# A gated delta layer on one NeuronCore: the TensorE order of a slot written as a list, and two products moved to four 64x64 tiles

## The chip, the cores and the metric

The program runs on one core of a Trainium2 chip. All data is float32. The metric is the device time of one execution in microseconds (us); the kernel before is given by the median of three runs.

## What is computed

Two layers over 2 sequences of 1024 tokens, 256 channels each. Layer 0 adds a gated delta rule and a mixture of experts to the stream; layer 1 adds a gated linear attention and a sparse unit. Nearly all the time goes to the delta rule of layer 0, and the change is there. Cut to what matters:

```python
qkvz = hidden_states @ W_qkvz                 # 16 key heads; each feeds 2 of the 32 value heads
q, k, v = silu(conv4(q, k, v))                # causal, 4 taps, per channel
q, k = l2norm(q) * 128**-0.5, l2norm(k)
def step(S, inp):                             # S: 128 x 128 per value head
    qt, kt, vt, gt, bt = inp
    S = S * exp(gt)
    delta = (vt - kt @ S) * bt
    S = S + outer(kt, delta)
    return S, qt @ S
gated = core * silu(z)
out = rms_norm(gated) * norm_w @ W_out
```

## The kernel before

Tokens of both sequences share the 128 partitions: the lower 64 hold 64 tokens of sequence 0, the upper 64 the same tokens of sequence 1. Such a block of 64 + 64 tokens is a chunk; there are 16 along the sequence. Heads go in 8 groups of four value heads (two key heads, `m` = 0 and 1, with two value heads `i` each), one group after the other, so there are 128 chunks of work. Two chunks make a pair (64 pairs), four a unit.

Inside a chunk the recurrence is solved in matrix form (`chunk_state`, L733): `pks`, `pqs` = keys and queries times the state (L748); DVE folds `pks` into the value tokens `vtok` (L751); `pf` = the inverted 64x64 triangle `invT` times `vtok` (L766), copied by ACT to `f` (L768); `pS` = keys times `f`, added to the state `S` by DVE (L775, L786); `po` = the query scores `np[:, 1]` times `f` (L779), added by DVE to `qs` (L790) and multiplied by the gate `z` (L792). ACT then takes four sums of squares (`gsq`, L797), POOL makes the norm's factors and multiplies (`chunk_output`, L807 to L814), and TensorE transposes and projects (`yT` L818, `out` L830). In `pf` the stationary and moving tensors span all 128 partitions: `invT` is a 128x128 matrix with the two sequences' 64x64 blocks on its diagonal and zeros elsewhere. `po` runs on two 64x64 tiles of the array, sequence 0 in the lower corner, sequence 1 in the upper. `pS` runs on all four.

The tokens' side (`chunk_tokens`, L707): TensorE transposes keys (`pk`) and values (`pv`), ACT copies the keys to `kt` (L716), and one POOL instruction scales them for four heads into `ktok` (L720).

The triangle of a pair is made in three steps spread over two slots. `pair_scores` (L521): DVE scans the decays (L540), ACT takes the exponential (L542), POOL multiplies (`lb`, L544), TensorE makes the scores `kq` (L552), DVE multiplies into `np` (L558; index 0 for the triangle, 1 for the outputs). SP then issues the DMAs that lay `np[:, 0]` out anew: `nat` (4, L562), `natd` to DRAM (2, L568) and from there `n` (8, L572). `pair_lanes` (L576): a chain of small DVE instructions inverts the 8x8 blocks of `n` (L590 to L612), ending in `E` (L614), which two DMAs turn into `U` by way of DRAM (`ed` L616, `U` L618). `pair_inverse` (L642), one slot later: DVE transposes `U` to `L` (L663); then twice TensorE `px`, ACT `xs`, TensorE `pyt` (L635), DVE `U` and `L` (L675, L677) join the blocks to 32x32, and once more `px`, `xs`, `pyt` (L692 to L703) to 64x64 in `invT`.

The work is a software pipeline over slots, one slot per pair: slot `p` makes the scores and lanes of pair `p`, the inverse of pair `p - 1`, both chunk states of pair `p - 2`, the last output of pair `p - 3`, and four blocks of projection and convolution (`conv_block`, L328: TensorE `pj`, ACT two copies L357 and L359, DVE three taps L376, ACT the silu L386). What sets the order of a slot is `in_windows` (L855): every piece of work is a generator with a window of the slot, and the piece whose next step is due first is advanced. A scheduler of the recording layer then orders each engine's instructions and puts in the semaphores; it follows these priorities but may exchange instructions that do not depend on each other. Engines take their instructions in order. SP's queue holds nearly all DMA issues, in one order as well, each waiting there for its data.

PSUM is one pool of eight banks, taken in turn by every product (`ps_tile`, L67).

Of the kernel before, what the change touches and what calls it, by code (L numbers as in the profile page):

```python
# [14 lines left out]
P = 128  # L15
D = 256
KT = D // P
NB = 2
# [162 lines left out]
def delta_gates(k, pool, I):  # L181
# [66 lines left out]
    for b, rows in enumerate((LO, HI)):  # L248
        ps = ps_tile(k, f"sum_end{b}")
        nc.tensor.matmul(ps, k.ones[rows], flat(g)[rows], start=True, stop=True)  # L250
        nc.scalar.activation(flat(k.eEnd[:, b]), ps, AF.Exp)
        yield
# [136 lines left out]

def conv_part(k, pools, p, n, count):  # L390

    u, odd = divmod(p, 2)
    blocks = []
    if odd:
        blocks = [(u + 1, 1, 0), (u + 1, 1, 1), (u + 1, 0, 2), (u + 1, 0, 3)]
    else:
        blocks = [(u + 1, 0, 0), (u + 1, 0, 1), (u, 1, 2), (u, 1, 3)]
    for v, m, i in blocks[n : n + count]:  # L400
        if 0 <= v < NUNIT:
            yield from conv_block(k, pools, k.units[v], m, i)
        elif k.projected:
            yield from convolve(k)
            silu_pending(k)
# [115 lines left out]
def pair_scores(k, pools, pr):  # L521

    nc, wk, h = k.nc, pools.work, pr.h
    pr.nat = wk.tile([P, PC, HPG, B], F32, tag="nat32", name=f"nat32{pr.name}")
    pr.n8 = wk.tile([P, W, W], F32, tag="n8", name=f"n8{pr.name}")

    lb, c0 = pr.g, pr.chunks[0].c
    flat = lb.rearrange("p x h i -> p (x h i)")
    with k.tc.issue_after(k.anchor):
        nc.vector.tensor_tensor_scan(flat, flat, k.floor, -200.0, ALU.add, ALU.max)  # L540
    yield
    nc.scalar.activation(flat, flat, AF.Exp)  # L542
    yield
    nc.gpsimd.tensor_tensor(lb, lb, bcast(h.nb[:, c0 : c0 + PC], 3, CT), ALU.mult)  # L544
    yield

    kq = ps_tile(k, f"kq{pr.name}").rearrange("p (x m s i) -> p x m s i", x=PC, m=KPG, s=2)
    for x in pr.chunks:
        for m in range(KPG):
            for b, rows in enumerate((LO, HI)):  # L550
                both = of_chunk(h.kq[m], x.c, b)
                nc.tensor.matmul(kq[rows, x.at, m], both[:, 0], both, start=True, stop=True)  # L552
    yield
    pr.np = pools.np.tile([P, 2, PC, HPG, CT], F32, tag="np", name=f"np{pr.name}")
    pairs = lambda a: a.rearrange("p x (m j) i -> p (x m) j i", m=KPG)
    for s in range(2):
        by = kq[:, :, :, s].rearrange("p x m i -> p (x m) i")
        nc.vector.tensor_tensor(pairs(pr.np[:, s]), pairs(lb), bcast(by, 2, 2), ALU.mult)  # L558
        if s == 0:
            yield  # L560
    for n, r in enumerate(QUARTERS):
        nc.sync.dma_start(pr.nat[r], pr.np[r, 0, :, :, QUARTERS[n % 2]])  # L562


    step = W * (PH * CT + 1)
    nd = k.dram.tile([NB, CT // W * step], F32, tag="nat", name=f"natd{pr.name}", bufs=2)
    for b, rows in enumerate((LO, HI)):
        nc.sync.dma_start(nd[b, 0 : CT * PH * CT].rearrange("(j c) -> j c", j=CT), pr.np[rows, 0].rearrange("p x h i -> p (x h i)"))  # L568
    for a in range(PH):
        at = slice(a * (P // W), (a + 1) * (P // W))  # L570
        src = bass.AP(nd.tensor, nd.offset + a * CT, [[step, P // W], [PH * CT, W], [1, W]])
        nc.sync.dma_start(pr.n8[at], src)  # L572
    yield
# [68 lines left out]
def pair_inverse(k, pools, pr):  # L642
# [42 lines left out]
    for n, r in enumerate(QUARTERS):  # L685
        (nc.gpsimd.tensor_copy, nc.scalar.copy)[n % 2](invT[r, :, r], U[r])
    yield
# [14 lines left out]
    for q, copy in ((0, nc.scalar.copy), (2, nc.vector.tensor_copy)):  # L702
        copy(invT[QUARTERS[q], :, QUARTERS[q + 1]], pyt[QUARTERS[q]])  # L703
    yield


def chunk_tokens(k, pools, x):  # L707

    nc, wk, h, c = k.nc, pools.work, x.h, x.c
    if not x.last:  # L710
# [6 lines left out]
        x.k = wk.tile([P, HPG, P], F32, tag="ktok", name=f"ktok{x.name}")  # L717
        pair = lambda a: a.rearrange("p (m i) c -> p m i c", m=KPG)
        wend = h.wend[:, c, :].rearrange("p (m i) -> p m i", m=KPG)
        nc.gpsimd.tensor_tensor(pair(x.k), bcast(kt, 2, 2), bcast(wend, 3, P), ALU.mult)  # L720
        yield
# [11 lines left out]
def chunk_state(k, pools, x):  # L733

    nc, wk, h, c = k.nc, pools.work, x.h, x.c
    t = h.t0 + c
# [4 lines left out]
    if not x.first:  # L741
        pks, pqs = four(k, f"pks{x.name}"), four(k, f"pqs{x.name}")
        for s, out in ((0, pks), (1, pqs)):
            for m in range(KPG):
                two = slice(2 * m, 2 * m + 2)
                for b, rows in halves:
                    q = of_chunk(h.kq[m][:, s], c, b)
                    nc.tensor.matmul(out[rows, two, :], q, k.S[:, b, two, :], start=True, stop=True)  # L748
        yield
# [13 lines left out]

    pf = four(k, f"pf{x.name}")
    for i in range(HPG):
        nc.tensor.matmul(pf[:, i, :], invT[:, i, :], x.v[:, i, :], start=True, stop=True)  # L766
    f = wk.tile([P, HPG, P], F32, tag="f", name=f"f{x.name}")
    nc.scalar.copy(f, pf)  # L768
    yield
    if not x.last:  # L770
        pS = [four(k, f"pS{x.name}_{b}") for b in range(NB)]
        for i in range(HPG):
            for b, rows in halves:
                for cols in (LO, HI):
                    nc.tensor.matmul(pS[b][cols, i, :], x.k[rows, i, cols], f[rows, i, :], start=True, stop=True)  # L775
    po = four(k, f"po{x.name}")
    for i in range(HPG):
        for b, rows in halves:
            nc.tensor.matmul(po[rows, i, :], x.pair.np[rows, 1, x.at, i, :], f[rows, i, :], start=True, stop=True)  # L779
    yield  # L780
# [6 lines left out]
    yield  # L787
    no = po
    if not x.first:
        nc.vector.tensor_tensor(qs, qs, po, ALU.add)  # L790
        no = qs
    nc.vector.tensor_tensor(x.z, no, x.z, ALU.mult)  # L792
    yield
# [77 lines left out]


def delta_layer(k, I):
    nc, tc = k.nc, k.tc
    with ExitStack() as ctx:
# [11 lines left out]
        k.tails = const.tile([P, 4 * KPG, NB, KSIZE - 1], F32, tag="tails", name="tails")  # L887
        k.invT = [const.tile([P, PC, HPG, P], F32, tag=f"invT{i}", name=f"invT{i}") for i in range(2)]

# [35 lines left out]
        for p in range(-2, NPAIR + 3):  # L925


            work = []
            add = lambda kind, lo, hi, steps, *before: work.append((kind, lo, hi, steps, before))
            prefetch(k, pools, p)  # L930
            if p == -2:
                for q in (0, 1):
                    pair_decays(k, pools, pair(q))
            add("conv0", 0.0, 0.475, conv_part(k, pools, p, 0, 2))
            add("conv1", 0.475, 0.71, conv_part(k, pools, p, 2, 1), "conv0")
            add("conv2", 0.71, 0.95, conv_part(k, pools, p, 3, 1), "conv1")
            add(f"gates{p % 2}", 0.65, 1.0, gates_part(k, pools, p), "output1", "conv1")
            if pair(p):
                add("scores", 0.0, 0.45, pair_scores(k, pools, pair(p)))
                add("lanes", 0.65, 0.9, pair_lanes(k, pools, pair(p)), "scores")  # L940
            if pair(p - 1):
                add("inverse", 0.0, 1.0, pair_inverse(k, pools, pair(p - 1)))
                add("tokens0", 0.5, 1.0, chunk_tokens(k, pools, pair(p - 1).chunks[0]), "state0")
            if pair(p - 2):
                one, two = pair(p - 2).chunks
                add("tokens1", 0.0, 0.4, chunk_tokens(k, pools, two))
                add("state0", 0.0, 0.5, chunk_state(k, pools, one))
                add("state1", 0.5, 1.0, chunk_state(k, pools, two), "state0", "tokens1")
                add("output0", 0.55, 1.0, chunk_output(k, pools, one), "state0")
            if pair(p - 3):  # L950
                one, two = pair(p - 3).chunks
                add("output1", 0.05, 0.5, chunk_output(k, pools, two))
                add("project0", 0.05, 0.4, chunk_project(k, pools, one))
                add("project1", 0.55, 0.9, chunk_project(k, pools, two), "output1")
            in_windows(k, *work)
            if pair(p) and pair(p + 2):
# [433 lines left out]
def two_layers(ctx, tc, I, out):  # L1390
# [3 lines left out]
    k.keep = ctx.enter_context(tc.tile_pool(name="keep", bufs=1))  # L1394
    k.psum = ctx.enter_context(tc.tile_pool(name="psum", bufs=8, space=bass.MemoryType.PSUM))

# [8 lines left out]
    k.xnT = k.keep.tile([P, KT, N], F32, tag="xnT", name="xnT")  # L1405

    with tc.tile_pool(name="ln0", bufs=2) as pool:
        tiles = {}
# [10 lines left out]
    with ExitStack() as scope:  # L1419
        k.gates = scope.enter_context(tc.tile_pool(name="d_gates", bufs=1))  # L1420
        k.dram = scope.enter_context(tc.tile_pool(name="d_dram", bufs=1, space=bass.MemoryType.DRAM))
        expert_layer(k, I)
        delta_layer(k, I)

    with ExitStack() as scope:
        pool = lambda name, bufs: scope.enter_context(tc.tile_pool(name=name, bufs=bufs))
        pools = Pools()
        pools.const, pools.work, pools.h = pool("l1_const", 1), pool("l1_work", 2), pool("l1_h", 2)
# [68 lines left out]
```

## Time and profile before

| | us |
|---|---|
| median of 3 runs (lowest, highest) | 2921.37 (2916.87, 2931.51) |
| the profiled execution, its time | 2925.03 |
| its span, first to last instruction | 2923.3 |
| first `pj` of the delta stage, from the timeline | 268.2 |
| last `out` of the delta stage | 2616.4 |
| first `kq` of slot 4, of slot 61, and 57 slots between | 420.7, 2468.1, 35.9 each |

PE is TensorE's matmuls, PEld its weight loads, DVE VectorE, ACT ScalarE, POOL GpSimd, SP the engine whose queue issues DMAs. A group's row has its line, engine, operation, output <- inputs, shape and count; then the union of its busy time in us, the mean of one instruction in ns, and the idle time of its engine before it with what ended it. A float32 matmul is two records, so counts are twice those of the source. Matmuls of different tiles overlap, so the busy time over the count is the price of one, and the mean is not.

### The profile page before, as it was taken

What the parts mean: (1) busy time and instruction counts of PE and PEld (TensorE: products, weight loads), DVE (VectorE), ACT (ScalarE), POOL (GpSimd) and SP (SyncE); (2) the same over time, 40 slices, a digit from 0 to 9 for tenths busy, and PEclk for the clock granted to TensorE, in tenths of its full rate; (3) what the DMA queues carried; (4) which work ended last, traced back from release to release, by engine and by line L of the source; (5) the groups of instructions that cost most, each with busy time, mean ns of one, the idle gap of its engine ahead of it and who ended that gap; (6) DMA issues with size and microseconds to landing.
All of it is one profiled execution on the core that took longest, in us unless ns stands there. A gap on an engine that the chain in (4) does not pass through costs nothing.

```text
span 2923.3 us, 87736 instructions
## 1 busy us (share of the span) xinstructions
PE 2657.6 (91%) x36502; PEld 1676.2 (57%) x36502; DVE 2000.5 (68%) x3845; ACT 1717.9 (59%) x4121; POOL 1608.1 (55%) x2690
## 2 busy tenths in 40 slices
PE   5998699999999999999999999999999999889997
PEld 2444455666566566656665666556665666554565
DVE  7653667777777777777767777777677777545544
ACT  4432666676666666766666667666666666544321
POOL 2222566676666666766676667666766666530000
PEclk9999899999999999999999999999999999999999
DMA  3001111111112111111111112111111111110000
GB/s 77 4 1 58 37 28 35 36 44 26 42 29 46 28 43 35 36 28 43 35 38 26 43 36 45 25 42 37 38 28 35 29 29 28 21 60 0 1 15 15
DMA packets 265965, 95.22 MB, mean 33 GB/s; under 512 B 220512, under 2 KB 244192, under 8 KB 265568
## 3 DMA queue, kind: packets, MB, share of 16 engines
q1 hardware_dynamic: 261872, 86.67, 13.3%
q8 instruction: 287, 4.70, 0.7%
q10 hardware_dynamic: 3696, 2.95, 0.4%
q14 instruction: 110, 0.90, 0.1%
HBM read 53.63 MB, written 27.53 MB: 28 GB/s over the span
## 4 chain that ended last, share of the span: by engine, by line
PE 55%; DVE 21%; POOL 9%; issue 6%; ACT 5%; DMA 3%; SPq 2%; DVEq 0%; ACTq 0%; POOLq 0%
PE pj L152 10%; DVE conv L376 5%; PE out L830 5%; PE z L152 3%; PE pks L748 3%; PE px L635 3%; PE pS L775 2%; PE pf L766 2%; PE pqs L748 2%; DVE S L786 2%; PE y L1115 2%; PE pg L152 2%; PE base L152 2%; DVE np L558 2%; POOL rn L479 2%
## 5 line engine op out<-in xcount | busy, mean ns | idle before, releaser
L376 DVE SCALAR_TENSOR_TENSOR conv<-raw,convw,conv 128x512 f32<-128x512 f32 x768 | 697.1, 938 | 22.2 <-ACT conv L359 18.7
L152 PE MATMUL pj<-xnT,w 128*128 128x512 f32 x1024 | 531.2, 645 | 9.4 <-DMA w<-in_W_qkvz 9.4
L797 ACT ACTIVATE gsq<-z 128x128 f32<-128x128 f32 x512 | 157.4, 307 | 352.3 <-DVE z L792 319.8
L756 POOL TENSOR_TENSOR S<-S,eEnd 128x512 f32<-128x512 f32 x224 | 274.4, 1244 | 75.8 <-PE pqs L748 46.0
L152 PEld LDWEIGHTS pj<-xnT,w 128*128 128x128 f32 x1024 | 192.4, 201 | 195.7 <-issue 186.5
L751 DVE SCALAR_TENSOR_TENSOR vtok<-pks,neG,vtok 128x128 f32<-128x128 f32 x480 | 135.2, 344 | 189.6 <-PE pks L748 188.7
L152 PE MATMUL z<-wz,xnT 128*128 128x512 f32 x512 | 260.3, 633 | 0.0
L830 PE MATMUL out<-wo,yTs 128*128 128x256 f32 x1024 | 250.7, 388 | 1.4 <-ACT yTs L820 1.4
L357 ACT COPY raw<-pj 128x512 f32<-128x512 f32 x256 | 146.3, 572 | 120.8 <-PE pj L152 81.1
L786 DVE TENSOR_TENSOR S<-S,pS 128x512 f32<-128x512 f32 x224 | 145.5, 682 | 84.6 <-POOL S L756 55.0
L830 PEld LDWEIGHTS out<-wo,yTs 128*128 128x128 f32 x1024 | 185.7, 191 | 25.6 <-ACT yTs L820 2.0
L635 PE MATMUL px<-L,natm 32*32 32x32 f32 x8192 | 99.8, 197 | 90.4 <-DVE L L677 73.5
L359 ACT ACTIVATE conv<-pj,convw 128x512 f32<-128x512 f32 x256 | 176.1, 688 | 0.0
L361 POOL COPY tails<-raw 128x6 f32<-128x6 f32 x192 | 52.0, 271 | 223.8 <-ACT raw L357 180.9
L386 ACT ACTIVATE v<-conv 128x512 f32<-128x512 f32 x128 | 81.1, 634 | 149.0 <-DVE conv L376 149.0
L761 ACT ACTIVATE qs<-pqs,neG 128x128 f32<-128x128 f32 x480 | 136.0, 362 | 42.9 <-PE pqs L748 42.8
L479 POOL TENSOR_TENSOR rn<-sse,mhalf 128x16 f32<-128x16 f32 x32 | 93.0, 2906 | 115.9 <-DVE sse L492 115.9
L635 PEld LDWEIGHTS px<-L,natm 32*32 32x32 f32 x8192 | 85.8, 108 | 115.9 <-DVE L L677 55.8
L807 POOL TENSOR_TENSOR ms<-sumsq,q 128x4 f32<-128x4 f32 x128 | 61.5, 480 | 160.8 <-ACT gsq L797 160.8
L720 POOL TENSOR_TENSOR ktok<-kt,wend 128x512 f32<-128x512 f32 x120 | 149.7, 1247 | 0.1
L152 PEld LDWEIGHTS z<-wz,xnT 128*128 128x128 f32 x512 | 92.5, 195 | 96.0 <-issue 72.9
L766 PE MATMUL pf<-vtok,invT 128*128 128x128 f32 x1024 | 143.9, 284 | 3.3 <-DVE vtok L751 3.3
(323 smaller groups left out, 6120.9 us busy)
## 6 DMA issues: line engine op xcount, KB each, us to landing
lb<-grows SPq DMA_DIRECT2D x128, 128.0 KB
natd<-np SPq DMA_DIRECT2D x128, 128.0 KB
w<-in_W_qkvz SPq DMA_DIRECT2D x16, 512.0 KB
nat<-np SPq DMA_DIRECT2D x256, 32.0 KB
n<-natd SPq DMA_DIRECT2D x512, 4.0 KB
ed<-E SPq DMA_DIRECT2D x64, 128.0 KB
U<-ed SPq DMA_DIRECT2D x64, 128.0 KB
wz<-in_W_qkvz SPq DMA_DIRECT2D x16, 256.0 KB
```

What stands on the lines that cost most here:

```text
L152: last = k.nc.tensor.matmul(ps, lhsT_of(kt), rhs_of(kt), start=(kt == 0), stop=(kt == KT - 1)).ins
L357: nc.scalar.copy(chunks(raw[:, :, KSIZE - 1 :]), pv)
L359: nc.scalar.activation(chunks(y), pv, AF.Copy, scale=tap(KSIZE - 1))
L376: k.anchor = k.nc.vector.scalar_tensor_tensor(y, shifted, tap(j), y, ALU.mult, ALU.add).ins
L479: nc.gpsimd.tensor_tensor(out, x, k.mhalf[:, 0 : x.shape[1]], ALU.pow)
L635: k.nc.tensor.matmul(out[r, i, :], lhsT[r, i, :], rhs[r, i, :], start=True, stop=True)
L720: nc.gpsimd.tensor_tensor(pair(x.k), bcast(kt, 2, 2), bcast(wend, 3, P), ALU.mult)
L756: nc.gpsimd.tensor_tensor(k.S[:, b], k.S[:, b], bcast(k.eEnd[:, b, t, h.h0 : h.h0 + HPG], 2, P), ALU.mult)
L766: nc.tensor.matmul(pf[:, i, :], invT[:, i, :], x.v[:, i, :], start=True, stop=True)
L786: nc.vector.tensor_tensor(k.S[:, b], k.S[:, b], pS[b], ALU.add)
L797: nc.scalar.activation(sq, x.z[:, i, :], AF.Square, accum_out=x.sumsq[:, i : i + 1])
L830: nc.tensor.matmul(po[:, 0:D], x.yT[:, i, :], wo[:, i, :], start=(i == 0), stop=(i == HPG - 1))
```

## The change

Six edits in one:

1. `SLOT` writes a slot's order as two lists of names, half a slot each. For each name one step of that piece of work is taken; at the end of a half the pieces in `DONE` are run out. During this `tc.manual_schedule(engines={PE})` keeps TensorE's instructions in exactly this order; the other engines are ordered by the scheduler as before. `in_windows` is not used for these slots any more.
2. `pf` and `po` are each eight products of 64x64 tiles, on all four tiles of the array. Key head 0 goes to the same half of the partitions as its input, key head 1 crosses to the other half (`across`). `invT` holds only the 64x64 blocks.
3. So the two key heads' results of a sequence lie in different halves: the state `S` and the decays `eEnd` of head 1 are stored with the halves exchanged (`b ^ m`), and head 1's keys and scores have to lie in the other half too. DVE makes the second half of `np[:, 1]` in an extra tile and two DMAs carry it across; the one POOL instruction of `ktok` becomes two of half the size, one of them into `ktoko`, which two DMAs carry across.
4. `pf` and `po` share one PSUM tile `fo` of two banks, one per key head, with one buffer; six banks stay for all other products.
5. PSUM pools are opened for the stage before, the delta stage and the stage after, in place of one for all.
6. `conv_part` yields all four blocks of a slot as one piece.

```diff
-    for s in range(2):
-        by = kq[:, :, :, s].rearrange("p x m i -> p (x m) i")
-        nc.vector.tensor_tensor(pairs(pr.np[:, s]), pairs(lb), bcast(by, 2, 2), ALU.mult)
-        if s == 0:
-            yield
+    by = kq[:, :, :, 0].rearrange("p x m i -> p (x m) i")
+    nc.vector.tensor_tensor(pairs(pr.np[:, 0]), pairs(lb), bcast(by, 2, 2), ALU.mult)
+    yield
+    other = wk.tile([P, PC, 2, CT], F32, tag="npo", name=f"npo{pr.name}", bufs=1)
+    for m, out in enumerate((pr.np[:, 1, :, 0:2], other)):
+        two = slice(2 * m, 2 * m + 2)
+        nc.vector.tensor_tensor(out, lb[:, :, two], bcast(kq[:, :, m, 1], 2, 2), ALU.mult)
+    for rows, across in ((LO, HI), (HI, LO)):
+        nc.sync.dma_start(pr.np[across, 1, :, 2:4], other[rows])
...
-        nc.gpsimd.tensor_tensor(pair(x.k), bcast(kt, 2, 2), bcast(wend, 3, P), ALU.mult)
+        other = wk.tile([P, 2, P], F32, tag="ktoko", name=f"ktoko{x.name}")
+        for m, out in ((1, other), (0, x.k[:, 0:2])):
+            wend = h.wend[:, c, 2 * m : 2 * m + 2]
+            nc.gpsimd.tensor_tensor(out, bcast(kt[:, m], 1, 2), bcast(wend, 2, P), ALU.mult)
+        for rows, across in ((LO, HI), (HI, LO)):
+            nc.sync.dma_start(x.k[across, 2:4], other[rows])
...
-                    nc.tensor.matmul(out[rows, two, :], q, k.S[:, b, two, :], start=True, stop=True)
+                    nc.tensor.matmul(out[rows, two, :], q, k.S[:, b ^ m, two, :], start=True, stop=True)
...
-    pf = four(k, f"pf{x.name}")
-    for i in range(HPG):
-        nc.tensor.matmul(pf[:, i, :], invT[:, i, :], x.v[:, i, :], start=True, stop=True)
+    fo = k.psum2.tile([P, KPG, 2, 2, P], F32, tag="fo", name=f"fo{x.name}")
+    pf, po = fo[:, :, 0], fo[:, :, 1]
+    across = lambda r, m: halves[r ^ m][1]
+    for i in range(2):
+        for m in range(KPG):
+            for r, rows in halves:
+                n = 2 * m + i
+                nc.tensor.matmul(pf[across(r, m), m, i, :], invT[rows, n, :], x.v[rows, n, :], start=True, stop=True)
...
-    po = four(k, f"po{x.name}")
-    for i in range(HPG):
-        for b, rows in halves:
-            nc.tensor.matmul(po[rows, i, :], x.pair.np[rows, 1, x.at, i, :], f[rows, i, :], start=True, stop=True)
+    for i in range(2):
+        for m in range(KPG):
+            for r, rows in halves:
+                n = 2 * m + i
+                nc.tensor.matmul(
+                    po[across(r, m), m, i, :], x.pair.np[rows, 1, x.at, n, :], f[rows, n, :], start=True, stop=True
+                )
...
+SLOT = (
+    """inverse state0 state0 output1 inverse scores tokens1 tokens1 tokens1 tokens1 tokens1 state0
+    conv inverse conv state0 scores state0 output1 conv conv conv state0 scores inverse conv
+    project0 state0 scores conv output1 inverse scores conv scores""",
+    """state1 state1 output0 inverse tokens0 tokens0 tokens0 tokens0 tokens0 state1 conv inverse conv
+    state1 state1 output0 lanes conv conv conv state1 lanes gates conv lanes project1 state1 lanes gates
+    gates output0 lanes gates conv gates lanes gates conv""",
+)
+DONE = {
+    SLOT[0]: {"state0", "scores", "tokens1", "output1", "project0"},
+    SLOT[1]: {"inverse", "state1", "tokens0", "output0", "project1", "lanes", "conv", "gates"},
+}
...
-        k.invT = [const.tile([P, PC, HPG, P], F32, tag=f"invT{i}", name=f"invT{i}") for i in range(2)]
+        k.invT = [const.tile([P, PC, HPG, CT], F32, tag=f"invT{i}", name=f"invT{i}") for i in range(2)]
...
-            add("conv0", 0.0, 0.475, conv_part(k, pools, p, 0, 2))
-            add("conv1", 0.475, 0.71, conv_part(k, pools, p, 2, 1), "conv0")
...
-                add("output1", 0.05, 0.5, chunk_output(k, pools, two))
-                add("project0", 0.05, 0.4, chunk_project(k, pools, one))
-                add("project1", 0.55, 0.9, chunk_project(k, pools, two), "output1")
-            in_windows(k, *work)
+                work["output1"] = chunk_output(k, pools, two)
+                work["project0"], work["project1"] = chunk_project(k, pools, one), chunk_project(k, pools, two)
+            with tc.manual_schedule(engines={mybir.EngineType.PE}):
+                for half in SLOT:
+                    for kind in half.split():
+                        next(work.get(kind, iter(())), None)
+                    for kind in half.split():
+                        if kind in DONE[half]:
+                            for _ in work.get(kind, ()):
+                                pass
...
-        delta_layer(k, I)
+        early.close()
+        with psum("psum1", 6) as k.psum, psum("psum2", 1) as k.psum2:
+            delta_layer(k, I)
```

## The prediction

> **What bounds the kernel now.** First the page, then the busy time of each engine over 57 steady slots, each 2047.4 / 57 = 35.92 us long.
>
> ```profile
> PE 2657.6 (91%) x36502; PEld 1676.2 (57%) x36502; DVE 2000.5 (68%) x3845; ACT 1717.9 (59%) x4121; POOL 1608.1 (55%) x2690
> ...
> 420.70:2468.10 2047.40, 1907.36 (x30770) 1242.04 (x30768) 1517.38 (x2884) 1354.46 (x3370) 1386.15 (x2329) 0.97 0.16 35
> ```
>
> Per slot TensorE is busy 33.46 us and idle 2.46; DVE is busy 26.62 and idle 9.3, POOL busy 24.3, ACT 23.8. TensorE is the bound, but DVE has only 9.3 us per slot to lose. Next, the groups of products to be changed, beside `pS`, which already uses four tiles:
>
> ```profile
> L766 PE MATMUL pf<-vtok,invT 128*128 128x128 f32 x1024 | 143.9, 284 | 3.3 <-DVE vtok L751 3.3
> L779 PE MATMUL po<-f,np 64*64 64x128 f32 x2048 | 135.2, 269 | 0.0
> L775 PE MATMUL pS<-f,ktok 64*64 64x128 f32 x3840 | 132.5, 275 | 8.0 <-ACT f L768 8.0
> ```
>
> Busy time over count is 140.5 ns a record for `pf`, 66 for `po` on two tiles, 34.5 for `pS` on four. Then the waits of the whole span, for what DVE's idle time is:
>
> ```profile
> DVE vtok L751 <- PE pks L748: 188.7, 92, 5.6
> ...
> DVE L L663 <- DMA U<-ed: 89.6, 62, 4.4
> ...
> PE px L635 <- DVE L L677: 73.5, 64, 4.1
> ```
>
> Last, the timelines of SP, POOL and DVE between 1528 and 1566 us, about one slot; times are start and duration:
>
> ```profile
> 1530.48 2.66 SPq L562 DMA_DIRECT2D nat<-np  x4
> 1533.19 1.25 SPq L568 DMA_DIRECT2D natd<-np  x2
> 1534.53 1.19 SPq L628 DMA_DIRECT2D lb<-grows  x2
> 1536.28 4.12 SPq L572 DMA_DIRECT2D n<-natd  x8
> 1551.56 0.34 SPq L616 DMA_DIRECT2D ed<-E  x1
> 1553.32 0.38 SPq L618 DMA_DIRECT2D U<-ed  x1
> ```
> ```profile
> 1537.97 0.65 POOL L807 TENSOR_TENSOR ms<-sumsq,q 128x4 f32<-128x4 f32 x1
> ...
> 1541.92 1.04 POOL L814 TENSOR_TENSOR z<-z,rms 128x512 f32<-128x512 f32 x1
> ...
> 1543.07 2.48 POOL L756 TENSOR_TENSOR S<-S,eEnd 128x512 f32<-128x512 f32 x2
> 1545.51 1.04 POOL L720 TENSOR_TENSOR ktok<-kt,wend 128x512 f32<-128x512 f32 x1
> 1546.49 1.79 POOL L686 COPY invT<-U 32x256 f32<-32x256 f32 x2
> ```
> ```profile
> 1529.77 1.28 DVE L558 TENSOR_TENSOR np<-lb,kq 128x512 f32<-128x512 f32 x2 [1.57 <-PE kq L552]
> ...
> 1551.11 0.42 DVE L614 TENSOR_TENSOR E<-X,place 128x256 f32<-128x256 f32 x1
> ...
> 1555.65 0.45 DVE L663 STREAM_TRANSPOSE L<-U 128x256 f32<-128x256 f32 x1 [1.14 <-DMA U<-ed]
> ```
>
> From `np` to `n` it is SP's issuing that counts, 0.5 to 0.7 us a DMA in one queue, and from the end of `E` (1551.53) to `L` the two DMAs take 4.12 us. TensorE's next `px` of that pair starts only at 1564.9, 9 us after `L`: this path, `kq` to `px`, has room before (36 us of TensorE's order).
>
> **The change, part by part.** *Four tiles.* `pf` goes from 1.12 us a chunk (143.9 / 128) and `po` from 1.06 to 16 records x 34.5 ns = 0.55 each: 1.08 us less a chunk, 2.16 a slot, 138 us over 128 chunks. Here the Trainium skill speaks against the change: "TensorEngine Tiling", Gotcha 1 (PSUM Pressure), says that different row tiles cannot access one PSUM bank at the same time, and in `fo` both row tiles write each key head's bank. By the rule the gain is 0. By the row, `po` has both row tiles in one bank already and costs half of `pf` a record, so they do overlap. I take the row: TensorE's work becomes 31.3 us a slot.
>
> *Side costs.* The second `np` product is two half-size ones at about 0.41 (the `U` add's size) for 0.68: +0.14 us of DVE a slot. `ktok` is two of 128x256: 0.5 to 0.8 each (half of 1.04 at the low end, `natm`'s mean of 0.80 at the high), so up to +0.6 us of POOL a chunk. SP gets six more issues a slot, 4 us on a queue with some 11 us of issues. Six PSUM banks plus `fo` for eight: `fo` must be read by the `qs` add before the next `pf`, some 8 us later in the list, so 0; 30 products a slot on six banks leave 7.2 us each where 34 on eight left 8.4; 0 taken, 0.5 us a slot at most, where a late `res` add holds a bank. Two more pool borders, 0 to 5 us in all: 0 taken, since 9.4 us of weight loading cover the first. Larger set-up edits are single instructions.
>
> *The list.* It moves every TensorE step. I added up, between dependent steps, the start-to-start times of TensorE's timeline (pk 0.37, pv 0.53, `pj` 1.91, `px` 0.68, `pyt` 0.68, `out` and gates 1.82, `kq` 1.02, `pks` 0.91, `pqs` 0.96). From the start of `kq` to the same pair's first `px` there are now only 20 to 21 us. The built program's order on the other engines, which the scheduler has adapted, gives what must pass in between and after, and it closes into a loop from one slot to the next:
>
> 1. First `px`, then pk, pv, `pf`, `pj`, `pyt` in TensorE's order: 0.68 + 0.37 + 0.53 + 0.48 + 1.91 + 0.68 = 4.65 us. DVE has nothing in its order between `L` (L663) and the `U` add that waits for this `pyt`; it stands idle.
> 2. DVE: `U`, `L`, two taps, two `S` adds, a tap, `qs`, a tap, `z`: 0.86 + 4 x 0.82 + 1.28 + 0.68 + 0.69 = 6.8 (taps between 0.74, one alone, and 0.94, the mean: 6.5 to 7.3).
> 3. ACT's four squares: 1535.41 to 1537.12, 1.7.
> 4. POOL: `ms` to `z`, 5.0 by the rows above, 4.1 without the tail copy and slow starts, 4.7 taken; `invT` 1.8, `S` 2.45, then `ktoko` 0.65: 9.6 (8.4 to 10.1).
> 5. SP, which before had nothing of POOL's ahead of `n`, now has the two `ktoko` DMAs there, between `natd` and `n`. It waits, and behind it stand `lb`, the eight `n`, `ed` and `U`: 1.3 + 0.6 + 4.1, and 1.4 until DVE can start on `n` (1540.40 to 1541.82): 7.4 (7.0 to 8.6, the longest where DVE waited for `n`).
> 6. DVE's lanes and `E`, now in one run: nine groups of rows sum to 2.5, `E` 0.6: 3.1 (2.8 to 3.6).
> 7. `E` to `L` 4.1, `L` 0.45: 4.6, and TensorE starts `px`.
>
> The sum is 37.85 us (35.5 to 40.6 with all ends together). Without the `ktoko` wait `n` would be issued some 4 us sooner and DVE itself sets the pace: its work 26.62 + 0.14, idle 4.65 in step 1, 2.7 in step 7 (4.1 less the 1.4 us of `res` and `vtok` put there), and 1.85 where the first tap of the next block waits for ACT's silu, copy, `invT` and scaling (0.53 + 0.47 + 0.38 + 0.69, less one DVE copy): 35.96. TensorE alone needs 31.3. The largest decides: 37.85, which is 1.93 more than before, and TensorE waits at `px` although it has less to do. All 64 pairs have a `ktoko` there; 60 slots are counted in full, since the stage's ends have less work: +116 us. The span of 2923.3 becomes 3039; with the 1.7 us around it and the 3.7 by which the profiled run (2925.0) lies above the median (2921.4), 3037 us.
>
> **The rivals.** *A: the `ktoko` wait hides and DVE's order sets the pace.* For it: step 4 with its low ends gives POOL's tile 1.2 us sooner, and taps at 0.74 free DVE sooner too. Against: `ms` waits for `gsq` in the present trace as well (160.8 us). 35.96 a slot is 2924 us, within 0.5% of before; the ends of its waits, 0.7 us a slot, make 2880 to 2970.
>
> *B: TensorE stays the bound and the gain is kept.* It needs the loop, both of its forms, to close in less than TensorE's slot. With the idle time of now, 2.46, a slot is 33.8, 2.2 less: 60 x 2.2 = 132, 2790 us. For it: the loop sum has 7 steps, each from rows taken under other overlap, and TensorE is the busiest engine by far. Against: DVE's 26.8 of work leaves 7.0 for waits, and steps 1 and 7 alone are 7.35. This decides from a loop of 35.7 down, where the kernel becomes faster by over 0.5%.
>
> *C: the four tiles do not overlap,* as the skill's rule has it. TensorE's slot is then 33.5, still below the loop; the time stays 3037 in my case, and in B it would be that of before.
>
> **How the numbers follow.** The loop through POOL and SP decides: 0.60 (its own range 2960 to 3120, loop 36.6 to 39.2); of this 0.56 slower, 0.03 the same, 0.01 faster. A: 0.22, with 0.10 slower, 0.07 the same, 0.05 faster. B: 0.18, all faster; C lies inside these. A measurement of this kernel tells 0.5% (15 us) from no change. Sums: faster 0.24, same 0.10, slower 0.66. The range from 2850 to 3140 leaves out most of B (0.15) and the slowest loops (0.05).
>
> **What would show it.** Right: `pf` and `po` at about 35 ns a record; TensorE idle 5 to 7 us a slot, nearly all before `px` L643, ended by DVE's `L` (L671); DVE idle before that `L` for the `U` DMA and before the `U` add for `pyt`; on SP a wait of the `ktok` issue for POOL, and DVE's first lane copy waiting for `n`. Wrong: idle TensorE under 3 us a slot (B); no DVE wait for `n` with DVE idle about 9 us (A); `pf` at 66 ns or more (C). If TensorE waits for a PSUM bank instead, the cost put at nothing was the wrong one.

## The result, and the profile after

| | before | after |
|---|---|---|
| median, four runs each on the same chip, us | 2919.9 | 3028.2 (3025.5 to 3030.7) |
| ratio to before, 95% interval | 1 | 1.0369 (1.0353 to 1.0384) |
| span of the profiled execution, us | 2923.3 | 3023.8 |
| first `pj` of the delta stage, us | 268.2 | 263.0 |
| last `out` of the delta stage, us | 2616.4 | 2717.6 |

The changed kernel is 3.7% slower: 3028 us where 3037 was predicted. The span of the profiled execution grew by 100.5 us. The delta stage grew by 106.4 (2454.6 for 2348.2); what lies ahead of it became 5.2 us shorter, what follows 0.7.

First the page's row of engine shares, then 57 steady slots, in the columns of the prediction's first fence:

```profile
PE 2586.0 (86%) x37526; PEld 1577.4 (52%) x37526; DVE 1855.7 (61%) x3909; ACT 1732.2 (57%) x4123; POOL 1566.6 (52%) x2810
```
```profile
427.10:2571.20 2144.10, 1843.17 (x31681) 1151.50 (x31680) 1377.19 (x2939) 1368.67 (x3371) 1345.69 (x2438) 0.94 0.19 44
```

A slot now takes 2144.1 / 57 = 37.62 us, 1.70 more than before. TensorE is busy for 32.34 us of it, 1.1 less than before, and idle for 5.28. DVE is busy for 24.2. No engine is busy throughout, so what sets the slot is a chain of waits. The groups of the changed products:

```profile
L788 PE MATMUL fo<-vtok,invT 64*64 64x128 f32 x2048 | 103.0, 319 | 0.0
L804 PE MATMUL fo<-f,np 64*64 64x128 f32 x2048 | 79.7, 270 | 1.1 <-ACT f L792 1.1
L799 PE MATMUL pS<-f,ktok 64*64 64x128 f32 x3840 | 133.4, 276 | 10.8 <-issue 4.5
```

Busy time over count is 50 ns a record for `pf` and 39 for `po`, for 140.5 and 66 before; `pf` has twice as many records as before, `po` the same number. The four tiles do overlap, and 279 us of products became 183. No product of `fo` waited for its PSUM tile: the idle time before `pf` is 0.0. Then the waits of the whole span (total, times, longest), and the SP queue's own:

```profile
DVE U L683 <- PE pyt L643: 360.2, 64, 7.8
...
PE px L643 <- DVE L L671: 262.4, 48, 20.6
...
DVE L L671 <- DMA U<-ed: 146.9, 63, 4.1
DVE X L598 <- DMA n<-natd: 138.7, 57, 6.5
...
DVE vtok L767 <- PE pks L764: 47.9, 24, 2.9
```
```profile
SPq L732 <- POOL ktoko L730: 583.1, 112, 12.1
```

TensorE's `px` waited 73.5 us for DVE before (for the second `L`), and now 262.4 for the first. DVE waits for `pyt`, for `U` and for `n`, and SP waits for POOL's `ktoko` (583.1 us for the transfers of both chunks; what lies ahead of `n` is counted below). One slot on SP (start, duration):

```profile
1524.93 0.65 SPq L570 DMA_DIRECT2D nat<-np  x1
1525.68 1.30 SPq L568 DMA_DIRECT2D np<-npo  x2
1527.03 2.82 SPq L570 DMA_DIRECT2D nat<-np  x3
1529.89 1.25 SPq L576 DMA_DIRECT2D natd<-np  x2
1532.34 1.13 SPq L732 DMA_DIRECT2D ktok<-ktoko  x2
1533.57 0.54 SPq L636 DMA_DIRECT2D lb<-grows  x1
1534.22 4.96 SPq L580 DMA_DIRECT2D n<-natd  x8
1539.22 0.47 SPq L636 DMA_DIRECT2D lb<-grows  x1
1543.04 0.34 SPq L624 DMA_DIRECT2D ed<-E  x1
1544.76 0.38 SPq L626 DMA_DIRECT2D U<-ed  x1
```

POOL and DVE over the same stretch:

```profile
1525.10 0.20 POOL L834 TENSOR_TENSOR ms<-sumsq,q 128x4 f32<-128x4 f32 x1 [1.94 <-ACT gsq L824]
...
1528.85 1.04 POOL L841 TENSOR_TENSOR z<-z,rms 128x512 f32<-128x512 f32 x1
1529.83 1.66 POOL L694 COPY invT<-U 32x256 f32<-32x256 f32 x2
...
1531.70 0.61 POOL L730 TENSOR_TENSOR ktoko<-kt,wend 128x256 f32<-128x256 f32 x1
```
```profile
1540.44 0.20 DVE L598 COPY X<-n 128x4 f32<-128x4 f32 x1 [2.13 <-DMA n<-natd]
...
1542.58 0.42 DVE L622 TENSOR_TENSOR E<-X,place 128x256 f32<-128x256 f32 x1
...
1547.07 0.45 DVE L671 STREAM_TRANSPOSE L<-U 128x256 f32<-128x256 f32 x1 [3.97 <-DMA U<-ed]
```

`natd` is issued by 1531.14, and SP then stands until `ktoko` ends at 1532.31. In this slot POOL has no `S` to scale ahead of `ktoko` (it falls out at a head group's first and last chunk), so the wait is short. Two slots earlier it is as long as in most:

```profile
1452.48 1.25 SPq L576 DMA_DIRECT2D natd<-np  x2
1457.68 1.13 SPq L732 DMA_DIRECT2D ktok<-ktoko  x2
1459.56 3.84 SPq L580 DMA_DIRECT2D n<-natd  x8
```
```profile
1454.60 2.04 POOL L772 TENSOR_TENSOR S<-S,eEnd 128x512 f32<-128x512 f32 x2
1456.60 1.06 POOL L730 TENSOR_TENSOR ktoko<-kt,wend 128x256 f32<-128x256 f32 x1
```

Over 55 slots SP's gap from the end of `natd` to the first `n` is 4.98 us in the mean, and 3.07 of that passes before `ktok` is issued. The eight `n`, the lanes, `E`, two more DMAs and `L` follow in order, and only then can TensorE start `px`.

### The profile page after: what moved, and what is told of

The parts are those of the page before. It is cut to its first block, busy times and chain, and to the rows that moved or that the text cites. A ratio compares the mean times of both kernels' runs of the same rounds, so it can differ in the third digit from the quotient of the medians.

```text
span 3023.8 us, 90468 instructions
## 1 busy us (share of the span) xinstructions
PE 2586.0 (86%) x37526; PEld 1577.4 (52%) x37526; DVE 1855.7 (61%) x3909; ACT 1732.2 (57%) x4123; POOL 1566.6 (52%) x2810
## 4 chain that ended last, share of the span: by engine, by line
PE 49%; DVE 14%; DMA 10%; POOL 8%; ACT 8%; SPq 6%; issue 5%; DVEq 0%; ACTq 0%; POOLq 0%
PE pj L152 12%; SPq L580 5%; DMA U<-ed 4%; DVE conv L379 3%; PE out L857 3%; PE px L643 3%; DMA n<-natd 3%; DMA ed<-E 3%; PE pS L799 2%; PE pyt L643 2%; PE fo L788 2%; PE y L1158 2%; PE pv L736 2%; PE pg L152 2%; PE base L152 2%
## 5 line engine op out<-in xcount | busy, mean ns | idle before, releaser
L379 DVE SCALAR_TENSOR_TENSOR conv<-raw,convw,conv 128x512 f32<-128x512 f32 x768 | 615.1, 811 | 35.2 <-DMA wz<-in_W_qkvz 13.7
L643 PE MATMUL px<-L,natm 32*32 32x32 f32 x8192 | 104.5, 202 | 298.1 <-DVE L L671 262.4
L152 PEld LDWEIGHTS pj<-xnT,w 128*128 128x128 f32 x1024 | 186.3, 202 | 194.1 <-issue 184.4
L683 DVE TENSOR_TENSOR U<-U,pyt 128x256 f32<-128x256 f32 x128 | 53.6, 418 | 360.2 <-PE pyt L643 360.2
L772 POOL TENSOR_TENSOR S<-S,eEnd 128x512 f32<-128x512 f32 x224 | 232.5, 1059 | 2.0 <-PE pqs L764 0.6
L364 POOL COPY tails<-raw 128x6 f32<-128x6 f32 x192 | 84.7, 453 | 240.7 <-ACT raw L360 240.7
L351 POOL COPY raw<-tails 128x6 f32<-128x6 f32 x192 | 108.0, 562 | 171.7 <-DVE conv L379 166.5
L679 ACT COPY xs<-px 128x256 f32<-128x256 f32 x128 | 47.5, 371 | 189.6 <-PE px L643 189.6
L152 PEld LDWEIGHTS z<-wz,xnT 128*128 128x128 f32 x512 | 99.4, 205 | 87.2 <-issue 84.7
L834 POOL TENSOR_TENSOR ms<-sumsq,q 128x4 f32<-128x4 f32 x128 | 25.8, 202 | 228.6 <-ACT gsq L824 228.6
L799 PE MATMUL pS<-f,ktok 64*64 64x128 f32 x3840 | 133.4, 276 | 10.8 <-issue 4.5
```

What stands on the lines that cost most here:

```text
L152: last = k.nc.tensor.matmul(ps, lhsT_of(kt), rhs_of(kt), start=(kt == 0), stop=(kt == KT - 1)).ins
L379: k.anchor = k.nc.vector.scalar_tensor_tensor(y, shifted, tap(j), y, ALU.mult, ALU.add).ins
L643: k.nc.tensor.matmul(out[r, i, :], lhsT[r, i, :], rhs[r, i, :], start=True, stop=True)
L772: nc.gpsimd.tensor_tensor(k.S[:, b], k.S[:, b], bcast(k.eEnd[:, b, t, h.h0 : h.h0 + HPG], 2, P), ALU.mult)
L799: nc.tensor.matmul(pS[r][cols, i, :], x.k[rows, i, cols], f[rows, i, :], start=True, stop=True)
```

## The experiments

The theory is the prediction's loop: POOL's `ms` to `ktoko`, `ktok` and `n` on SP, lanes, `E`, `U`, `L`, `px`, `pyt`, `U`, `z`, `gsq`, and `ms` again, once a slot. The main rival is that engine orders set the pace, whether or not `ktok` stands ahead of `n`. Before measured 2921.5 to 2923.2 us beside these runs. A slot in this part is a mean over 56 slots, from the first `kq` of slot 4 to that of slot 60; counted so, before has 35.92 us and the changed kernel 37.56.

| run | us | ratio to before (95% interval) |
|---|---|---|
| n first | 2900.0 | 0.9915 (0.9894 to 0.9937) |
| pyt early | 2963.8 | 1.0144 (1.0129 to 1.0160) |
| list alone | 2911.5 | 0.9963 (0.9950 to 0.9976) |
| tiles alone | 2958.3 | 1.0124 (1.0109 to 1.0139) |
| filler | 3036.8 | 1.0401 (1.0374 to 1.0427) |
| kq first | 3067.6 | 1.0494 (1.0476 to 1.0512) |
| six banks | 2911.3 | 0.9966 (0.9952 to 0.9979) |
| npo late | 2888.5 | 0.9882 (0.9861 to 0.9903) |
| tiles, npo late | 2937.1 | 1.0046 (1.0031 to 1.0061) |
| lanes late | 3010.1 | 1.0295 (1.0274 to 1.0316) |
| more POOL | 3120.9 | 1.0681 (1.0665 to 1.0697) |
| more POOL, n first | 2971.9 | 1.0170 (1.0153 to 1.0187) |

### n first: the ktok transfers behind n

```diff
-        nc.sync.dma_start(pr.n8[at], src)
+        k.laid = nc.sync.dma_start(pr.n8[at], src).ins
...
-            nc.sync.dma_start(x.k[across, 2:4], other[rows])
+            with k.tc.issue_after(k.laid):
+                nc.sync.dma_start(x.k[across, 2:4], other[rows])
```

> The changed kernel, with the ktoko DMAs put behind the eight n DMAs in SP's queue; TensorE, DVE, ACT and POOL keep their orders. Theory (the loop through POOL and SP sets the slot, step 5): in the changed kernel DVE waits 2.3 us a slot for n before its first lane copy; that wait goes, and the slot falls from 37.6 us to DVE's own order, 35.2 to 35.8, so 62 slots x 1.8 to 2.4 = 110 to 150 us less: 2880 to 2920 us. Rival (the slot is set by DVE's and TensorE's order alone, and the n wait only fills time that would be waited elsewhere, at L for U or at the U add): 3010 to 3030 us, with the DVE wait moved and not gone.

Measured: 2900.0 us, 128 less than the changed kernel and 0.85% under before. The slot is 35.56 us. The same stretch on SP:

```profile
1534.36 1.91 SPq L576 DMA_DIRECT2D natd<-np  x2
1536.37 1.19 SPq L636 DMA_DIRECT2D lb<-grows  x2
1538.11 3.63 SPq L580 DMA_DIRECT2D n<-natd  x8
1541.86 1.14 SPq L733 DMA_DIRECT2D ktok<-ktoko  x2
```
```profile
PE px L643 <- DVE L L671: 187.3, 59, 20.7
...
DVE X L598 <- DMA n<-natd: 11.1, 4, 6.6
```

From `natd`'s end to the first `n` it is now 1.89 us in the mean over 59 slots, 3.09 less; the slot gained 2.0 of it. DVE waits for `n` for 11.1 us in all, for 138.7. TensorE, ACT and POOL keep exactly the order of the changed kernel; on DVE `L` and one lane step change places with a neighbour in 23 slots. Two issues moved behind ten others in one DMA queue take back the whole loss and more. So the `ktok` issue ahead of `n` made the change slower.

### List alone and tiles alone: the change taken apart

The list alone is the kernel before with `SLOT`, its loop and `conv_part`; the products, PSUM and transfers of `np` and `ktok` stay as they were. The tiles alone keep everything else of the change under `in_windows`.

> The kernel before with the list alone: pf and po as before, nothing crosses halves, no ktoko and npo, eight PSUM banks in one pool. Theory (the list's 20 us from kq to px, against 36 before, makes the loop, and the ktoko wait is 2.3 us of it): slot about 35.2 + 0.5 to 1.0 for the longer pf in step 1 = 35.7 to 36.3, so 2910 to 2960 us, with TensorE idle at the first px. Rival (the tiles' side costs are what is lost, and the list by itself is a gain or nothing): 2800 to 2900 us. Rival (the list alone is the whole loss): 3020 us or more.

> The changed kernel without the list: four tiles, crossing DMAs, six banks and fo, but each slot ordered by due times as before. Theory (the loss is the list's; with 30 us and more from kq to px all of the POOL and SP path is covered): TensorE's 31.3 us and 2.5 to 3.5 idle, slot 33.8 to 34.8, 62 x 1.1 to 2.1 = 70 to 130 us under the kernel before: 2790 to 2850 us. Rival (six more SP issues, two banks less and the crossings cost as much anywhere): 2920 us or more.

```diff
+            with tc.manual_schedule(engines={mybir.EngineType.PE}):
+                for half in SLOT:
+                    for kind in half.split():
+                        next(work.get(kind, iter(())), None)
...
-            in_windows(k, *work)
```

Measured: the list alone is faster by 0.4% (slot 35.73 us), at the low end of what was expected. Beside it the run n first, which has the tiles too, gains only 11.5 us more, of the 96 us that the tiles take off TensorE. The tiles alone are slower by 1.2% (slot 36.55), where a gain of 70 to 130 us was expected. Under the planner (`in_windows`) nearly all `ktok` already stand behind `n`, so this loss has another source; the two runs below look for it.

### Six banks, and the tiles with the npo transfers late

```diff
-    k.psum = ctx.enter_context(tc.tile_pool(name="psum", bufs=8, space=bass.MemoryType.PSUM))
+    psum = lambda name, bufs: tc.tile_pool(name=name, bufs=bufs, space=bass.MemoryType.PSUM)
...
+        with psum("psum1", 6) as k.psum:
+            delta_layer(k, I)
```

> The kernel before with six PSUM banks in the delta stage instead of eight, and nothing else; the planner's order stays. Theory (the tiles alone lost because fo's two banks were taken from the other tiles' eight, so that TensorE's products wait for a bank): most of the 35 us between the tiles alone (2958) and before, 2940 to 2965 us. Rival (the loss is in the two added transfers, the split multiplies and SP): 2915 to 2930 us.

Measured: 2911.3 us, 0.34% faster than with eight banks and under both ranges, with every instruction in the same place on every engine. The edit opens the pools by stage as well, as the change does. So the prediction's 0 for the banks holds, and the tiles alone did not lose for want of them. TensorE's granted clock was 0.974 to 0.976, for 0.966 to 0.970 before; why was not tried.

```diff
-    for rows, across in ((LO, HI), (HI, LO)):
-        nc.sync.dma_start(pr.np[across, 1, :, 2:4], other[rows])
...
+    for rows, across in ((LO, HI), (HI, LO)):
+        with k.tc.issue_after(k.laid):
+            nc.sync.dma_start(pr.np[across, 1, :, 2:4], other[rows])
```

> The tiles alone under the planner (2958 us) with the same move of the two np<-npo transfers behind the n transfers. Six banks alone cost nothing (2911 us), so the 35 us between the tiles alone and before lie in the added transfers and split operations. Theory (they lie in what was put ahead of nat and natd, 1.3 to 1.9 us a slot, of which the tiles' own gain took some back): 2870 to 2920 us. Rival (they lie in the ktok wait on SP or in the two halves of the POOL and DVE multiplies): 2940 to 2970 us.

Measured: 2937.1 us, 21 less than the tiles alone, above the theory's range and just under the rival's. The two transfers ahead of `nat` are part of the loss. Some 15 us to before stay without a settled cause.

### npo late: the same move in the run n first

> The run n first (list and tiles, ktok behind n) with the two np<-npo transfers moved behind the n transfers too. Ahead of nat and natd they held SP for 2 x 0.63 us, and waited for npo's two halves on DVE (0.33 us each). Theory (with the ktok wait gone the slot is the loop kq, np, natd, n, X, E, U, L, px, kq): the loop loses 1.3 to 1.9 us in nearly every slot, 80 to 115 us in all: 2785 to 2830 us. If another loop stands close behind, half of it: 2830 to 2870. Rival (that loop doesn't set the slot, the additions, z, gsq and ms do): 2885 to 2915 us.

Measured: 2888.5 us, 11.5 less than the run n first; the slot is 35.48 us. That is in the rival's range. The loop from `kq` through `np`, `n`, `L` and `px` back to `kq` is not alone in setting the slot: taking two issues out of it on SP, 1.3 us by the shown row, shortened the slot by 0.08. It is still the fastest of all the kernels here, 1.2% under before.

### pyt early, kq first, lanes late: other orders on TensorE

Each starts from the run n first. The run pyt early takes the first `pyt` ahead of `pj`:

```diff
-    conv inverse conv state0 scores state0 output1 conv conv conv state0 scores inverse conv
+    inverse conv conv state0 scores state0 output1 conv conv conv state0 scores inverse conv
```

> As the run before, and in the first half of the list the first pyt stands ahead of the projection pj in place of behind it. Theory (step 1, in which DVE stands idle from L to the U add, is part of the loop): it shortens by that pj, which takes 1.9 us, or 2.7 at the clock granted after the long wait: 62 x 1.9 to 2.7 = 118 to 167 us under the run before, so 2730 to 2790 us if that one lies near 2900. Rival (DVE's idle time only moves to the next wait, or TensorE's 31.3 us of work and its other waits decide): within 30 us of the run before.

Measured: 2963.8 us, 64 more than the run n first. DVE's wait did shrink, and others grew:

```profile
POOL ms L835 <- ACT gsq L825: 324.1, 91, 8.6
...
DVE U L683 <- PE pyt L643: 237.0, 65, 4.8
...
ACT gsq L825 <- DVE z L820: 189.1, 119, 4.9
```

In the run n first these three are 229.1, 341.3 and 115.5. With the new list the scheduler also gave DVE and ACT another order: four taps ahead of the `S` additions where there were two, and the value silu ahead of the second `pj`'s copy. Which of the exchanges costs the 64 us was not separated. The trace says where it lies: a slot grew by 1.06 us, DVE's idle time in it did not (11.3 for 11.4), and its taps took 923 ns in the mean for 840, 1.0 us a slot. More of them now run beside a POOL instruction, which the part on more POOL takes up.

The run kq first takes all six `scores` steps ahead of the first `px`:

```diff
-    """inverse state0 state0 output1 inverse scores tokens1 tokens1 tokens1 tokens1 tokens1 state0
+    """inverse state0 state0 output1 scores scores scores scores scores scores inverse tokens1
```

> The list with the ktok transfers behind the n transfers (as in the run n first), and all six scores steps moved ahead of the first px, so that TensorE makes kq while it would wait for L, and nat, natd and n go out some 11 us earlier in the slot. Theory (with the ktok wait gone, the slot is the loop kq, np, natd, n 14.5 to 15.6 us, X to L 8.5 to 10.9 us, px to kq 10.7 to 12.2 us, which sums to 35.6; here the last part is cut out of it): the slot falls towards TensorE's own work of some 32 us, 33.0 to 34.5, so 2740 to 2840 us. Rival (the slot is set by the loop through DVE's additions, z, gsq, ms and the state, in which kq has no part): within 25 us of the run n first, 2875 to 2925 us. If the earlier np on DVE, or the second ktok, which now stands ahead of ed on SP, holds something else up: above 2925 us.

Measured: 3067.6 us, over 200 us above the theory's range: something is held up. DVE had got one lane copy, which waits for `n`, ahead of the `U` addition of the pair before:

```profile
DVE X L605 <- DMA n<-natd: 197.6, 52, 6.8
```

The run lanes late holds that copy behind the last tap:

```diff
-    nc.vector.tensor_copy(at(X, 0, 2, two, row), at(n, 0, 2, two, row))
+    with k.tc.issue_after(k.anchor):
+        nc.vector.tensor_copy(at(X, 0, 2, two, row), at(n, 0, 2, two, row))
```

> The run kq first (3068 us), in which DVE had one copy of X, which waits for n, ahead of the addition to U of the pair before, with this copy held behind DVE's last tap, so that the addition and the transpose stand ahead of all that waits for n. Theory (the run kq first lost because the new place of that copy closed a loop kq, n, X, U, L, px, kq over one slot, 36 to 40 us): the slot falls towards TensorE's own work, 33 to 35 us, 2740 to 2860 us. Rival (kq ahead of px is bad in itself: np and npo on DVE, or the second ktok ahead of ed): above 2950 us.

Measured: 3010.1 us. The copy was worth 57 us; 110 over the run n first remain. So `kq` ahead of `px` is worse in this program for reasons that one copy does not explain, and the theory's freed slot of 33 to 35 us did not come (37.6).

### Filler: TensorE kept busy before px

In the changed kernel TensorE runs slowly after its long stalls. Its timeline after a stall of 2.64 us, then after one of 7.67 us (in brackets: idle before it, and what ended it):

```profile
1472.08 0.74 PE L643 MATMUL px<-L,natm 32*32 32x32 f32 x64 [2.64 <-DVE L L671]
...
1473.04 0.60 PE L736 MATMUL pv<-ident,v 128*128 128x128 f32 x4
1473.57 0.67 PE L788 MATMUL fo<-vtok,invT 64*64 64x128 f32 x16
1474.16 1.98 PE L152 MATMUL pj<-xnT,w 128*128 128x512 f32 x4
1476.08 0.75 PE L643 MATMUL pyt<-U,xs 32*32 32x32 f32 x64
...
1510.09 1.08 PE L643 MATMUL px<-L,natm 32*32 32x32 f32 x64 [7.67 <-DVE L L671]
1511.10 1.11 PE L736 MATMUL pv<-ident,v 128*128 128x128 f32 x4
1512.14 1.13 PE L788 MATMUL fo<-vtok,invT 64*64 64x128 f32 x16
1513.21 3.26 PE L152 MATMUL pj<-xnT,w 128*128 128x512 f32 x4
1516.40 0.75 PE L643 MATMUL pyt<-U,xs 32*32 32x32 f32 x64
```

```diff
+def filler(k, p):
+    ps = ps_tile(k, f"fill{p}")
+    for _ in range(0 if p % 2 == 0 else 2 if p % 8 == 3 else 11):
+        k.nc.tensor.matmul(ps, k.ident, k.xnT[:, 0, 0:512], start=True, stop=True)
+    yield
```

> The changed kernel with TensorE work of no use in the wait before the first px: 128x512 products, 11 of them (11 x 0.478 us by the pj row = 5.3 us) in the slots in which px waited 7.4 to 8.2 us (odd p, not 3 modulo 8), 2 in those where it waited 3.7 us (p = 3 modulo 8), none in the others. In the trace of the changed kernel every px behind a stall of 3.6 us or more was followed by 12.0 to 13.5 us up to kq, every px behind a stall of 3.3 us or less by 10.67 us (or 8.40), with the same instructions between. Theory (the slow stretch is the lowered clock, and it lies on the loop): 28 slots lose 1.4 to 2.4 us each, some 50 us in all; with the filler px to kq is 10.7 us in nearly all slots, the mean clock of the stretch rises and the time falls to 2960 to 2995 us. Rival (the slow stretch lies in the shadow of the ktok wait on SP, which sets the slot whatever TensorE does): 3015 to 3040 us, with px to kq shorter all the same.

Measured: 3036.8 us, in the rival's range, and the mean clock rose from 0.936 to 0.972. But the filler was sized wrongly: a product is two records, so eleven take twice the 5.3 us of the expectation.

```profile
1503.06 9.71 PE L919 MATMUL fill<-xnT,ident 128*128 128x512 f32 x22
1512.69 0.75 PE L643 MATMUL px<-L,natm 32*32 32x32 f32 x64
```

In this slot `L` was ready at 1510.94, so `px` started 1.75 us late; over the 28 filled slots the lateness is 1.83 us in the median, for 0.15 in the changed kernel. In those slots `px` to `kq` fell by about as much, from 12.57 to 10.68 us. The one offset the other. In six of the seven slots with two products `px` to `kq` stayed at 12.1 to 12.3 us, though `px` was not late and the stall ahead of it was down to 1.8 to 3.2 us. The run shows that the slow stretch is the clock's, and leaves open what a warm clock alone would be worth.

### More POOL: the price of POOL's place in the loop

```diff
+            idle = wk.tile([P, 2 * P], F32, tag="idle", name=f"idle{x.name}", bufs=1)
+            for _ in range(2):
+                with k.tc.issue_after(last):
+                    last = k.idle = nc.gpsimd.tensor_tensor(idle, k.xnT[:, 0, 0:256], k.xnT[:, 1, 0:256], ALU.mult).ins
```

> The changed kernel with idle work on POOL between S and ktoko of every chunk: two multiplies of 128x256, together about as long as one of S's (128x512, 1.23 us). Nothing else moves. Theory (the slot of the changed kernel is the loop ms, z, S, ktoko on POOL, ktok and n on SP, X, E, U, L, px, pyt, U, z, gsq, ms, passed once a slot): all of it is added to the slot, 1.2 us x 60 = 74 us, 3090 to 3115 us. Rival (POOL is not on what sets the slot): 3020 to 3045 us.

> The same idle work on POOL in the run n first (2900 us), in which ktok stands behind n on SP. Theory (that move took POOL out of what sets the slot): little is added, 2895 to 2930 us. Rival (POOL still sets the slot through ktoko, by another way than n): 2960 to 2990 us.

Two idle multiplies took 1.72 us, not the 1.23 expected (group rows: 862 ns each, and 891 in the second run). In the changed kernel the time is 3120.9 us, just over the theory's range, which had counted on the shorter multiplies. The slot rose by 1.49 us to 39.05, and SP's gap from `natd` to `n` by 1.33 to 6.31: most of the rise came out at `n`. That is the theory's loop, at 0.86 of one chunk's addition.

In the run n first the gap stays at 1.90, and yet the slot rose by 1.18 us to 36.74, and the time is 2971.9 us: the rival's range. But its reason, a wait for `ktoko`, is not what the trace shows. First the 56 slots without and with the idle work, in the columns of the prediction's first fence, then DVE's scan of the decays in both:

```profile
422.52:2413.90 1991.38, 1784.32 (x31125) 1123.46 (x31125) 1353.96 (x2884) 1343.95 (x3312) 1318.60 (x2401) 0.97 0.21 46
424.93:2482.30 2057.37, 1793.38 (x31123) 1130.77 (x31122) 1420.33 (x2882) 1342.12 (x3311) 1505.02 (x2596) 0.95 0.20 45
```
```profile
L544 DVE TENSOR_TENSOR_SCAN lb<-lb,floor 128x512 f32<-128x512 f32 x64 | 77.7, 1213 | 0.0
L544 DVE TENSOR_TENSOR_SCAN lb<-lb,floor 128x512 f32<-128x512 f32 x64 | 100.1, 1563 | 0.0
```

DVE's order is the same in both runs. Its busy time (the third pair) rose from 24.18 to 25.36 us a slot, as much as the slot, and its idle time stayed at 11.38. So nothing is waited for longer: DVE's own instructions became longer. Over these slots the scan takes 1604 ns in the mean for 1213, `z` 851 for 681, `E` 689 for 455 and a tap 863 for 840. In each of these groups the instructions with no arithmetic of POOL running beside them (its TENSOR instructions, copies not counted) keep their old length; all that are much longer have some beside them. The idle work moved more of POOL's work beside them. In the run n first DVE's own order is then what every added us passes through, and POOL slows it from outside.

## Why the prediction was right

The time came out 9 us under the forecast, by the loop that it names; that it is as near as that is partly luck, since terms of the sum were off both ways. Step by step, medians over 50 slots of the changed kernel's trace:

| step | predicted, us | measured, us |
|---|---|---|
| 1 `L` to `U`'s addition | 4.65 | 5.60 |
| 2 DVE to `z` | 6.8 | 6.08 |
| 3 squares, and start of `ms` | 1.7 | 1.71 + 0.17 |
| 4 POOL `ms` to `ktoko` | 9.6 | 4.74 + 3.81 + 1.06 = 9.61 |
| 5 SP `ktok` to `n` landed | 7.4 | 1.88 + 3.41 + 1.85 = 7.14 |
| 6 lanes and `E` | 3.1 | 2.83 |
| 7 `E` to `L` | 4.6 | 4.10 + 0.45 = 4.55 |
| sum | 37.85 | 37.69 (slot 37.62) |

Single slots take 33 to 41 us, in a pattern of eight (one head group), so that medians added up can meet the mean slot only roughly.

- *The bound.* Right: TensorE has less to do and waits 5.3 us a slot, mostly at `px`, as said. The run n first shows the step that decides, `ktok` ahead of `n`, by taking it out.
- *Four tiles.* The row was the right guide and the Trainium skill's rule ("TensorEngine Tiling (Array Packing)", Gotcha 1) was not: two row tiles in one bank overlap. The gain was over-sized: 96 us for 138. Warm slots have 0.60 and 0.55 us a chunk from the start of one group to the next, for the 0.55 predicted; the products behind long stalls take up to 1.13.
- *Step 1 was too short* because the clock was taken as before (and `pf` at 0.48 us, where the prediction itself has 0.55). In 21 of 55 slots `px` waited 7.4 to 8.2 us, and what follows ran slowly: 7.0 us from `px` to `pyt`'s end in the slot shown, 4.7 in the warm one.
- *Step 2 was too long.* DVE's taps took 811 ns in the mean for 938 before (615.1 us for 697.1 over the same 768). With no arithmetic of POOL beside it a tap takes 731 ns before and 744 after; 172 taps ran so before, 405 after. No run separates what moved them apart. Steps 1 and 2 nearly cancel.
- *Step 4* is exact in sum only. `ktoko` is 0.80 us in the mean of its group and 1.06 in the loop's place, for 0.65; `invT` and `S` came out below their estimates.
- *Ends.* 57 slots gave 96.7 us, 9.7 more came from the stage's two ends, and 5.9 were won outside: 100.5 in the span (108 in the medians), where 60 x 1.93 = 116 was predicted.
- *Rival A* is what the kernel becomes without the wait: 35.96 us and 2924 were worked out for it, 35.56 and 2900 measured. Its reason, DVE's own order, fits: with more POOL work that slot grew by what DVE's instructions grew, at the same idle time. No run made DVE's work less, and why other orders on TensorE made the slot longer is shown in part only. *Rival B* did not occur in any run, nor did *C*.

## What to carry to other kernels

A DMA issue that waits for its data holds all that stand behind it in its queue. Before work is added to such a queue, ask what it waits for and what is behind it; here two transfers of 64 KB each, standing ahead of nine others, cost 128 us, more than the change saved on TensorE. When no engine is busy throughout, less work on the busiest one need not show in the time (here 1.1 us less of TensorE in a slot that grew by 1.7): add up the loop of dependent steps from one slot to the next, and test it by moving one wait. And when an order is changed on one engine, read what the scheduler did to the others before trusting a gain, and whether instructions of the others became longer, not only what they waited for.

## What the runs showed of the hardware

TensorE's granted clock falls in a long stall and stays low after it. In the trace's record of it the clock is 1 or 0.5, and in the delta stage the stretches at 0.5 last 3.4 us or a multiple of that. In the changed kernel all 27 slots with a stall of 3.3 us or less before `px` took 8.40 or 10.67 us from `px` to `kq`; all 28 with 3.6 us or more took 12.0 to 13.5, and in these the clock was back at 1 only 3.2 to 6.3 us after `px` had started. Behind the long stall `pv` took 1.11 us for 0.60 and `fo` 1.13 for 0.67, and `pyt`, 6.3 us after the restart, was back to 0.75. The length of the stall is not the whole rule: in the filler run the clock fell to 0.5 from 1581 to 1584 us, behind a stall of 1.82 us that followed two filler products. The Trainium skill ("TensorE: Matmul & The Clock Gate", Part 1) has half rate follow an idle window of about 3.4 us, and full rate a busy window of that length. The step of 3.4 us agrees with the traces; the fall behind a stall of 1.82 us does not. The profile's shares of busy time hide all this: slow products count as busy.

A DVE instruction can take longer beside POOL. Before, a tap took 731 ns in the mean with no arithmetic of POOL running beside it and 1004 with some beside it for half of its time or more; for `z` it was 691 and 1288. The additions to `S`, which read PSUM, took 678 and 685.

Six PSUM banks in place of eight, with an identical order on every engine, were 0.34% faster and not slower.
